# A two-layer attention block: the transfers of a unit's sums get a list of their own, and one load of layer 1's cross attention stands two rounds later

## The chip, the cores and the metric

The kernel runs on one core of a Trainium2 chip. The metric is the device time of one execution in microseconds; shown are the median and the spread of three runs. TensorE is called PE below, VectorE DVE, ScalarE ACT, GpSimd POOL and SyncE SP, as in the profile. SP computes nothing here: it issues the DMA transfers, one after the other, and a transfer whose data or buffer isn't ready holds up all that stand behind it.

## The reference

Input are x (4 batches of 512 tokens of 320 values) and a context (4 batches of 1601 tokens of 192 values), all in fp32. Two layers of the same form, with their own weights, follow each other. Of a layer, cut to what matters (20 heads of 16 values):

```
h1 = ln(x);  x = attn(h1, h1)      + x      # self attention, 512 keys
h2 = ln(x);  x = attn(h2, context) + x      # cross attention, 1601 keys
h3 = ln(x);  a, g = split(h3 @ ff_w1 + ff_b1)
x  = (a * gelu(g)) @ ff_w2 + ff_b2 + x

attn: q, k, v from wq, wk, wv;  softmax(q k^T / 4) v;  then @ wo + bo
```

## The kernel before, in words

**Units.** The work is cut into units. One unit of attention is a layer, a kind (self or cross), a batch b (0 to 3) and a group g of four heads (0 to 4, the 20 heads in fives of four). So each layer has 20 self units, then 20 cross units, then four feed-forward units, one for each batch. A unit takes its keys in chunks of 128: 4 chunks for self attention, 13 for cross attention (the last with 65 keys). For each chunk PE makes the scores of the four heads transposed (`st`, L1324), ACT takes the exponential into `pr` (L1334), and PE multiplies it with the values (`av`, L1350). The sums of the first chunk are copied to `o` by ACT (L1364); those of each later one are copied to `vo` (L1369) and added to `o` by POOL (L1370). The values have a column of ones, so `o` holds the softmax's denominators too. There are two `o` buffers, used in turn.

**Maxima one unit ahead.** While one unit is computed, PE also makes the scores of the next unit untransposed (`sps`, L1076 and L1101), and DVE takes their maxima (L1087, L1111). Two chunks before the unit ends the maxima are put together and transposed (`turned`, L1163), and four small transfers take them to `nrows` (L1171). The third `st` product of the next unit subtracts them, so its first chunk can't be finished before `nrows` has landed.

**The order of the work.** Nothing is scheduled by the chip: a planner in the kernel's Python code writes all instructions in one order, and each engine does its own in that order. It counts rounds: a chunk is two rounds. At each round it looks at the heads of several lists (`chains`), first in, first out, each entry with a due round and with conditions on rounds. `pick` takes, among the heads that may go, the one with the smallest due round, and the list's name decides between equal ones. The lists are for dividing, projecting, normalising and so on. Entries that cost PE time are also held back by a credit that is filled at an even pace. Transfers of queries and keys (L876) and of normalised rows (L595) come from lists of another kind and follow the picked work of a round.

**What follows a unit.** When a unit's last chunk is done, `add_finish` puts `turn` (L1191) in a list. It writes `o` from the chip to a buffer in memory (`oway`), 256 KB. After the fifth group of a batch, `sums` reads the denominators back (L1199), DVE inverts them, they are written out (L1208), and `read` loads numerators `aT` and inverse denominators `rT` (L1224, L1225) in three parts of 112, 112 and 96 rows; POOL multiplies them (`divide`, L1232). `rT` has two buffers: the third `rT` load waits until POOL has done the first division. Both of `turn` and of the divisions stand in the list "divide", so a `turn` waits in that list behind divisions and loads of the batch before. The third load may go when a number of rounds has passed since the second load: seven in layer 0, five in layer 1. Then comes the third division, and after it the projection with `wo` in eight pieces of 12 matmuls (`ops`, L1250), which DVE adds to x (L1257).

**Feed-forward.** The last batch of a layer's cross attention is divided and projected during the first feed-forward units. A feed-forward unit makes two matrix products into `fps` (L1435 for 256 of the 320 rows, L1495 for the rest), ACT and DVE make `hid` from them (L1506, L1507), and four products `yps` of 128 tokens (L1542) are added to x by DVE (L1549) and, in layer 1, written out by SP (L1553). Its input is normalised by DVE, transposed in blocks, moved by SP to `hT` in 16 transfers (L595) and scaled by POOL (L612).

Of the kernel before, what the change touches and what calls it, by code (L numbers as in the profile page):

```python
# [78 lines left out]
def kernel(ctx: ExitStack, tc: tile.TileContext, x, context, ws, out):  # L79
# [313 lines left out]

    chains = {n: deque() for n in ("divide", "project", "norm", "scale", "context", "early", "proj", "values")}
    clock = {"round": 0, "credit": 0.0, "lights": 0, "tiles": None, "ff": False}
    ALIKE = ("project", "early", "proj", "values")
    LIGHT = 0.01
# [13 lines left out]
    def bank(name):  # L413
        i = min(range(NB), key=lambda i: bank_free[i])
        assert bank_free[i] < HELD, name
        t = psum.tile([P, 512], F32, tag=f"bank{i}", name=name)
        bank_of[id(t)] = [i, t, bank_free[i], 0.0]
        bank_free[i] = HELD
        return t

    def written(us, *tiles):
        expect["pe"] = max([expect["pe"]] + [bank_of[id(t)][2] + 0.05 for t in tiles]) + us
        for t in tiles:
            bank_of[id(t)][3] = expect["pe"] + 0.17

    def busy(engine, us, *tiles):
        expect[engine] = max([expect[engine]] + [bank_of[id(t)][3] + 0.05 for t in tiles]) + us
        for t in tiles:
            bank_free[bank_of[id(t)][0]] = expect[engine] + 0.09
# [12 lines left out]
    def add(chain, cost, f, due, ready=yes, soon=yes):  # L442
        chains[chain].append((cost if isinstance(cost, tuple) else (cost,), due, ready, soon, f))
# [356 lines left out]
    def tiles_of(n):  # L800
        return [(f, min(SLOT, n - f)) for f in range(0, n, SLOT)]

    held = {"open": 0, "written": 0, "read": 0}
# [375 lines left out]
    def add_finish(u):  # L1179

        when = [clock["round"]]

        def since(i, n):
            return lambda: len(when) > i and clock["round"] >= when[i] + n

        def turn():

            way = o_way[u.b % 2]  # L1190
            dma(out=way[:, u.g * HG : (u.g + 1) * HG].rearrange("s j n -> j s n"), in_=u.o)  # L1191
            if u.g == G - 1:
                held["written"] += 1
                errands.append((clock["round"] + 3, yes, sums))

        def sums():

            den = two.tile([P, N], F32, tag="rT", name="den")[:, : H * N // P]
            dma(out=den, in_=o_way[u.b % 2][DH].rearrange("h n -> (h n)").rearrange("(p c) -> p c", p=P))  # L1199
            when.append(clock["round"])  # L1200

            def invert():
                nc.vector.reciprocal(den, den)
                busy("dve", 0.75)
                when.append(clock["round"])

            def save():
                dma(out=r_way[u.b % 2].rearrange("h n -> (h n)").rearrange("(p c) -> p c", p=P), in_=den)  # L1208
                errands.append((clock["round"] + 3, lambda: held["open"] < 1, read))

            add("divide", LIGHT, invert, r - 20, yes, since(1, 3))
            add("divide", 0.0, save, r - 20, yes, since(2, 1))

        def read():

            held["read"] += 1
            held["open"] += 1
            aT = one.tile([P, 3, N], F32, tag="aT", name="aT")
            way, part = o_way[u.b % 2], {}

            def load(k, at, n):
                heads = slice(at // DH, (at + n) // DH)
                part[k] = two.tile([P, N], F32, tag="rT", name="rT")
                dma(out=aT[:n, k, :], in_=way[:DH, heads])  # L1224
                dma(  # L1225
                    out=part[k][:n],
                    in_=r_way[u.b % 2][heads].rearrange("(o j) n -> o j n", o=1).to_broadcast([DH, n // DH, N]),
                )
                when.append(clock["round"])

            def divide(k, n):
                nc.gpsimd.tensor_tensor(aT[:n, k, :], aT[:n, k, :], part[k][:n], ALU.mult)  # L1232

            for k, at, n in DK[:2]:
                load(k, at, n)
            first, second, third = DK
            add("divide", 0.0, lambda: divide(0, first[2]), r - 20, yes, since(4, 3))
            add("divide", 0.0, lambda: divide(1, second[2]), r - 20)
            add("divide", 0.0, lambda: load(*third), r - 20, yes, since(4, 5 if u.l else 7))
            add("divide", 0.0, lambda: divide(2, third[2]), r - 20, yes, since(5, 3))  # L1240
            add("divide", 0.0, lambda: end(aT), r - 20)

        def project(aT, t, part):
            cols = slice(part * D // 2, (part + 1) * D // 2)
            ps = bank("ops")
            written(0.93, ps)
            busy("dve", 0.3, ps)
            for k, at, n in DK:
                for f, m in tiles_of(P):
                    nc.tensor.matmul(  # L1250
                        ps[f : f + m, : D // 2],
                        lhsT=aT[:n, k, f * NQ + t * SLOT : f * NQ + t * SLOT + m],
                        rhs=wo[:n, k, cols],
                        start=(k == 0),
                        stop=(k == 2),
                    )
            nc.vector.tensor_tensor(xs[u.b][:, t, cols], ps[:, : D // 2], xs[u.b][:, t, cols], ALU.add)  # L1257

        def end(aT):
            now = clock["round"]  # L1260
            for t in range(NQ):
                for part in range(2):
                    add(
                        "project", (0.317,) * 3, lambda t=t, part=part: project(aT, t, part),
                        now + 2 + u.nch * t + u.nch // 2 * part, yes, lambda: clock["round"] >= now + 1,
                    )
            add("project", 0.0, done, now + 2 + u.nch * NQ)

        def done():
            held["open"] -= 1  # L1270
            after(u)

        r = when[0]
        add("divide", 0.0, turn, r - 20, lambda: u.g or held["written"] < held["read"] + 2, since(0, 2))


    late = []
# [33 lines left out]
    def main(u, give, nxt):  # L1311
# [31 lines left out]
        def values(c):  # L1343
            r = min(P, u.nkeys - c * P)
            if u.g in (0, 2):
                until(lambda: units[u.i - u.g].vmade[u.g // 2] > c, "values")
            ps = bank("av")
            for j in range(HG):
                head = (c * H + u.g * HG + j) * VW
                nc.tensor.matmul(  # L1350
                    ps[j * SLOT : (j + 1) * SLOT, :],
                    lhsT=columns_of[:r, head : head + SLOT],
                    rhs=pr.pop((c, j))[:r, :],
                    start=True,
                    stop=True,
                )
            u.valued = c + 1
            expect["pe"] = max(expect["pe"], raised[c] + 0.1)
            written(1.0, ps)
            busy("dve" if last else "act", 0.52, ps)  # L1360

            if c == 0:
                u.o = two.tile([P, N], F32, tag="o", name="o")
                (nc.vector.tensor_copy if last else nc.scalar.copy)(u.o, ps)  # L1364
            elif last:
                nc.vector.tensor_tensor(u.o, ps, u.o, ALU.add)
            else:
                vo = prs.tile([P, N], F32, tag="pr", name="vo")
                nc.scalar.copy(vo, ps)  # L1369
                nc.gpsimd.tensor_tensor(u.o, u.o, vo, ALU.add)  # L1370
            if c == u.nch - 1:
                add_finish(u)
# [214 lines left out]
    def after(u):  # L1587

        stage[u.b] += 1
        if u.b == B - 1:  # L1590
            load_bias(u.l, ("self", "cross", "ff").index(u.kind) + 2)
            if u.kind == "self":
                loads.extend(load_out(u.l, "o2_w"))
            if u.kind == "cross" and u.l + 1 < L:
                loads.extend(load_out(u.l + 1, "o1_w"))
            if u.l + 1 < L:
                if u.kind == "ff":
                    loads.extend(load_cross(u.l + 1))
                elif u.kind == "self":
                    loads.extend(load_self(u.l + 1))  # L1600
# [172 lines left out]
```

## Time and profile before

| | |
|---|---|
| median of 3 runs | 2929.41 us (2924.77 to 2933.03) |
| the profiled execution, its own time | 2929.68 us |
| its span, first to last instruction | 2927.9 us |
| PE busy, share of the span | 2863.1 us (98%) |
| DVE, ACT, POOL busy | 1980.7, 1950.1, 1299.5 us |
| DMA, mean over the span | 64 GB/s |
| cross attention, layer 0 and layer 1 | about 424 to 1206 us and 1871 to 2650 us |

The page of the profile gives busy time by engine, and the chain of work that ended last. The waits tell for each engine which instruction sat idle and which event ended it: "PE st L1324 <- DMA nrows<-turned: 7.0, 8, 1.6" reads 7.0 us in all, 8 times, the longest 1.6 us. The waits of SPq are those of the DMA issuing queue. A row of the timeline is a start, a length, the engine and line, and what is written from what; "x4" means that four instructions were merged in the row, and brackets at its end give idle time before it and what ended it. A row of SPq shows the issue of a transfer, not its landing.

### The profile page before, as it was taken

The numbers are of one execution on the slowest core, as the hardware profiler recorded it, in microseconds if no ns is written. First come the engines' busy times: TensorE is split into PE (matmuls) and PEld (weight loads), VectorE is DVE, ScalarE is ACT, GpSimd is POOL, SyncE is SP. The second block draws the span as 40 slices with busy tenths as digits, with TensorE's granted clock in tenths as the row PEclk, the third lists the DMA queues.
The fourth block names the chain that finished last, engine by engine and source line by source line (L and its number), as shares of the span: only waits on it lengthen the run. The fifth ranks groups of instructions, "written<-read, shape, count | busy, mean of one in ns | idle before, by whom it ended". The sixth has DMA issues, their size and how long they took to land.

```text
span 2927.9 us, 83288 instructions
## 1 busy us (share of the span) xinstructions
PE 2863.1 (98%) x35018; PEld 1545.3 (53%) x35018; DVE 1980.7 (68%) x3752; ACT 1950.1 (67%) x4033; POOL 1299.5 (44%) x1409
## 2 busy tenths in 40 slices
PE   8999999999999999999999999999999999999999
PEld 4445555555555555355554555555555555544554
DVE  7776878788788878323257678788778888762221
ACT  3777678887888888500138776788888888893000
POOL 3556345555555645211125653455455564451110
PEclk8999999999999999999999999999999999999999
DMA  3443224232232222200113432221122122122000
GB/s 106 111 123 98 67 71 105 59 82 63 51 92 62 54 54 62 84 18 11 36 44 88 109 98 66 68 65 49 54 65 50 47 72 63 42 59 72 20 23 14
DMA packets 163494, 188.59 MB, mean 64 GB/s; under 512 B 61988, under 2 KB 109104, under 8 KB 163120
## 3 DMA queue, kind: packets, MB, share of 16 engines
q1 hardware_dynamic: 162616, 181.69, 24.3%
q8 instruction: 275, 4.51, 0.6%
q10 hardware_dynamic: 472, 1.58, 0.2%
q14 instruction: 99, 0.81, 0.1%
q0 software_dynamic: 32, 0.00, 0.0%
HBM read 55.76 MB, written 29.36 MB: 29 GB/s over the span
## 4 chain that ended last, share of the span: by engine, by line
PE 85%; DVE 6%; POOL 4%; issue 2%; DMA 2%; ACT 1%; SPq 1%; POOLq 0%; ACTq 0%; DVEq 0%
PE av L1350 21%; PE st L1324 19%; PE fps L1435 10%; PE sps L1076 8%; PE yps L1542 6%; PE vps L1035 5%; PE ops L1250 3%; PE kps L972 3%; PE qkps L908 3%; PE fps L1495 3%; DVE nmax L1087 2%; DVE pm L1087 2%; PE qps L947 2%; POOL o L1370 1%; PE sps L1101 1%
## 5 line engine op out<-in xcount | busy, mean ns | idle before, releaser
L1334 ACT ACTIVATE pr<-st 128x512 f32<-128x512 f32 (+1 forms) x2720 | 1404.5, 604 | 327.1 <-PE st L1324 297.0
L1087 DVE TENSOR_REDUCE pm<-sps 128x1 f32<-128x512 f32 (+1 forms) x1920 | 1149.0, 660 | 251.0 <-PE sps L1076 243.8
L1370 POOL TENSOR_TENSOR o<-o,vo 128x512 f32<-128x512 f32 x576 | 739.8, 1284 | 936.9 <-ACT vo L1369 922.1
L1076 PE MATMUL sps<-kT,q 32*128 32x450 f32 (+1 forms) x4800 | 870.7, 422 | 10.7 <-DMA q<-halves 4.3
L1324 PE MATMUL st<-q,kT 32*128 32x512 f32 (+1 forms) x5120 | 791.1, 420 | 2.0 <-ACT o L1364 1.6
L1350 PE MATMUL av<-pr,vals 128*32 128x512 f32 (+1 forms) x5440 | 734.8, 606 | 30.7 <-DVE pm L1087 7.2
L1324 PEld LDWEIGHTS st<-q,kT 32*128 32x128 f32 (+1 forms) x5120 | 448.6, 180 | 293.9 <-ACT pr L1334 115.4
L1324 PE MATMUL st<-nrows,ones 32*128 32x512 f32 (+1 forms) x2720 | 560.8, 398 | 7.1 <-DMA nrows<-turned 7.0
L1087 DVE TENSOR_REDUCE nmax<-sps 128x1 f32<-128x512 f32 x640 | 397.2, 682 | 120.6 <-PE sps L1076 115.2
L1076 PEld LDWEIGHTS sps<-kT,q 32*128 32x128 f32 x4800 | 434.6, 184 | 69.5 <-ACT pr L1334 12.8
L1369 ACT COPY vo<-av 128x512 f32<-128x512 f32 x576 | 352.9, 613 | 15.2 <-PE av L1350 8.5
L1506 ACT ACTIVATE gl<-fps,b 128x512 f32<-128x512 f32 x80 | 54.7, 687 | 409.0 <-PE fps L1495 301.1
L1435 PE MATMUL fps<-hT,w 128*128 128x512 f32 x640 | 283.5, 597 | 0.0
L1324 PEld LDWEIGHTS st<-nrows,ones 32*128 32x128 f32 (+1 forms) x2720 | 263.3, 180 | 18.7 <-issue 6.2
L1350 PEld LDWEIGHTS av<-pr,vals 128*32 128x32 f32 (+1 forms) x5440 | 110.9, 108 | 304.3 <-DVE pm L1087 186.7
L1507 DVE SCALAR_TENSOR_TENSOR hid<-fps,b,gl 128x512 f32<-128x512 f32 x80 | 59.7, 748 | 247.5 <-ACT gl L1506 245.4
L1435 PEld LDWEIGHTS fps<-hT,w 128*128 128x128 f32 x640 | 119.1, 190 | 155.0 <-issue 152.3
L1542 PE MATMUL yps<-w,hid 128*128 128x320 f32 x640 | 175.7, 434 | 0.0
L1542 PEld LDWEIGHTS yps<-w,hid 128*128 128x128 f32 x640 | 120.5, 190 | 56.3 <-ACT gl L1506 5.3
L1250 PEld LDWEIGHTS ops<-wo,aT 112*32 112x32 f32 (+1 forms) x3072 | 97.9, 110 | 61.9 <-issue 30.0
L1250 PE MATMUL ops<-wo,aT 112*32 112x160 f32 (+1 forms) x3072 | 124.9, 300 | 4.1 <-POOL aT L1232 3.8
L1111 DVE TENSOR_REDUCE pm<-sps 128x4 f32<-128x508 f32 x160 | 98.9, 681 | 36.1 <-PE sps L1101 33.0
(89 smaller groups left out, 2459.5 us busy)
## 6 DMA issues: line engine op xcount, KB each, us to landing
kT<-stages SPq DMA_DIRECT2D x80, 400.5 KB
oway<-o SPq DMA_DIRECT2D x80, 256.0 KB
q<-halves SPq DMA_DIRECT2D x80, 256.0 KB
q<-halves SPq DMA_DIRECT2D x27, 512.0 KB
kT<-halves SPq DMA_DIRECT2D x40, 256.0 KB
aT<-oway SPq DMA_DIRECT2D x32, 224.0 KB
rT<-rway SPq DMA_DIRECT2D x32, 224.0 KB
hT<-hturned SPq DMA_DIRECT2D x96, 64.0 KB
```

The costliest lines, as they stand in the source:

```text
L1035: nc.tensor.matmul(ps[f : f + m, :w], lhsT=u.kvT[:n, k, at + f : at + f + m], rhs=wv[:n, k, h0 * DH : h1 * DH], start=(k == 0), stop=(k == ...
L1076: nc.tensor.matmul(own[0][:, :w], lhsT=u.queries(slice(j * SLOT, (j + 1) * SLOT), e, t), rhs=u.kT[j * SLOT : (j + 1) * SLOT, u.k0 + at : u ...
L1087: nc.vector.tensor_reduce(to, own[0][:, :w], AX.X, ALU.max)
L1111: nc.vector.tensor_reduce(u.pm[:, :, j, ns - 1], ps[:, : NQ * w].rearrange("p (t w) -> p t w", w=w)[:, :, :n], AX.X, ALU.max,)
L1250: nc.tensor.matmul(ps[f : f + m, : D // 2], lhsT=aT[:n, k, f * NQ + t * SLOT : f * NQ + t * SLOT + m], rhs=wo[:n, k, cols], start=(k == 0) ...
L1324: nc.tensor.matmul(own[0][:r, :], lhsT=ones[rows, :r] if e == 2 else u.keys(rows, c), rhs=u.rows[rows, :] if e == 2 else u.queries(rows, e ...
L1334: nc.scalar.activation(p[:r], own[0][:r], AF.Exp)
L1350: nc.tensor.matmul(ps[j * SLOT : (j + 1) * SLOT, :], lhsT=columns_of[:r, head : head + SLOT], rhs=pr.pop((c, j))[:r, :], start=True, stop= ...
L1369: nc.scalar.copy(vo, ps)
L1370: nc.gpsimd.tensor_tensor(u.o, u.o, vo, ALU.add)
L1435: nc.tensor.matmul(ps, lhsT=w1[:, k, i * FF + c * P : i * FF + (c + 1) * P], rhs=natural(u.hT[:, k]), start=start, stop=stop,)
L1542: nc.tensor.matmul(ps[:, :D], lhsT=hid[c][:, t * P : (t + 1) * P], rhs=w2[:, c, :], start=(c == 0), stop=(c == NHC - 1),)
```

## The change

Two edits.

First, `turn` gets a list of its own, "turn", in place of the list "divide". Its due round and its conditions are the same. The new list is named first in the table of lists; `pick` goes by due round and then by name, so the place in the table doesn't decide.

Second, the third load of `aT` and `rT` waits seven rounds instead of five after the second load in the cross units of layer 1. Layer 1's self units keep five, layer 0 keeps seven.

```
-    chains = {n: deque() for n in ("divide", "project", "norm", "scale", "context", "early", "proj", "values")}
+    chains = {n: deque() for n in ("turn", "divide", "project", "norm", "scale", "context", "early", "proj", "values")}
...
-            add("divide", 0.0, lambda: load(*third), r - 20, yes, since(4, 5 if u.l else 7))
+            add("divide", 0.0, lambda: load(*third), r - 20, yes, since(4, 5 if u.l and not u.cross else 7))
...
-        add("divide", 0.0, turn, r - 20, lambda: u.g or held["written"] < held["read"] + 2, since(0, 2))
+        add("turn", 0.0, turn, r - 20, lambda: u.g or held["written"] < held["read"] + 2, since(0, 2))
```

What the two edits do to the order of the instructions can be told apart. The first moves instructions on SP alone, at six places: three in layer 0's self attention and three in layer 1's, each time one `turn` that now stands in front of transfers it stood behind. The second moves the third load on SP, and from there on, in layer 1's cross attention and in its feed-forward units, the rounds in which projections, key and value products and norms are placed. The number of instructions of each kind stays the same.

The first of the six places, on SP, in layer 0's self attention (some 177 us into the span): `aT`, `rT` are batch 0's third load, `oway_131` is written by the `turn` of a unit of batch 1. L765 saves the transposed context to memory, L779 loads it from there; the lines between the two pieces are the same in both kernels, and the four `nrows` of the next unit are among them, behind four L779 loads.

```order
 L1225 DMA rT<-rway_132 96x1x512
+L1191 DMA oway_131<-o 4x32x512
 L765 DMA ctxT_126<-stages 768x1x32
 L779 DMA w_116<-ctxT_126 96x1x416 x2
...
 L779 DMA w_116<-ctxT_126 96x1x385 x2
-L1191 DMA oway_131<-o 4x32x512
 L876 DMA kT_101<-halves 128x1x512
```

The `turn` now stands in front of the last context save, the context loads and the `nrows` of the next unit.

The second place, on SP, in the same stage (some 265 to 275 us): the third load of batch 1, and the `turn` of a unit of batch 2.

```order
 L876 DMA q_102<-halves 128x1x1024
-L1171 DMA nrows_97<-turned 8x4x32 x4
-L1224 DMA aT<-oway_131 96x1x512
-L1225 DMA rT<-rway_133 96x1x512
-L876 DMA kT_101<-halves 128x1x512
-L876 DMA q_103<-halves 128x1x1024
-L1191 DMA oway_130<-o 4x32x512
+L1191 DMA oway_130<-o 4x32x512
+L1171 DMA nrows_97<-turned 8x4x32 x4
...
 L1191 DMA oway_130<-o 4x32x512
```

The `turn` now stands in front of eight transfers that it stood behind. At the other four places (some 344, 1631, 1719 and 1794 us) it changes places with the four `nrows` that stood in front of it.

The third load in layer 1's cross attention, on SP, batch 0 (some 2064 to 2080 us); batch 1 and batch 2 show the same exchange.

```order
 L1225 DMA rT<-rway_132 112x1x512
-L1224 DMA aT<-oway_130 96x1x512
-L1225 DMA rT<-rway_132 96x1x512
-L1171 DMA nrows_97<-turned 8x4x32 x4
+L1171 DMA nrows_97<-turned 8x4x32 x4
+L1224 DMA aT<-oway_130 96x1x512
+L1225 DMA rT<-rway_132 96x1x512
 L1191 DMA oway_131<-o 4x32x512
```

The four `nrows` of the next unit now stand in front of the third load.

Behind that, each piece of the projection comes one chunk later on PE, or two come together, and key and value products move by a chunk to make room. In the feed-forward units of layer 1 the eight projection pieces of batch 3 also come later: the last two stood in batch 2's unit between the two halves of 16 L1435 products, and now stand behind these and the 8 L1495 products that follow. On SP, the 16 `hT` transfers of batch 3 were all in front of batch 2's four output transfers; now six stand in front of the first output, six between the first and the second, and four between the second and the third.

## The prediction

> **What bounds the kernel now.** I read the page first (busy shares and the chain of work that ended last), then PE's waits over the whole span, then PE's waits in each layer's cross attention, then the timeline at every place where the order of the instructions changes.
>
> ```profile
> span 2927.9 us, 83288 instructions
> PE 2863.1 (98%) x35018; PEld 1545.3 (53%) x35018; DVE 1980.7 (68%) x3752; ACT 1950.1 (67%) x4033; POOL 1299.5 (44%) x1409
> PE 85%; DVE 6%; POOL 4%; issue 2%; DMA 2%; ACT 1%; SPq 1%; POOLq 0%; ACTq 0%; DVEq 0%
> PE st L1324 <- DMA nrows<-turned: 7.0, 8, 1.6
> ```
>
> PE is busy for 2863.1 of 2927.9 us, so all that a new order can win at most, with the same PE work, is 64.8 us of idle time, and most of that lies in places that the change doesn't touch. A change in the order pays by the PE waits it ends or makes, and by nothing else. One kind of wait fits the change: PE waits eight times for `nrows`, 7.0 us in all. Next come the waits of PE in layer 1's cross attention (first four rows, 1870 to 2655 us) and in layer 0's (last five rows, 424 to 1206 us).
>
> ```profile
> PE av L1350 <- DVE pm L1087: 3.9, 6, 1.2
> PE st L1324 <- DMA nrows<-turned: 2.8, 3, 1.1
> PE av L1350 <- ACT pr L1334: 0.8, 4, 0.2
> PE sps L1076 <- ACT pr L1334: 0.5, 1, 0.5
> PE av L1350 <- DVE pm L1087: 3.3, 2, 2.0
> PE av L1350 <- ACT pr L1334: 2.3, 10, 0.3
> PE sps L1076 <- DVE x L1257: 0.7, 1, 0.7
> PE av L1350 <- ACT vo L1369: 0.3, 1, 0.3
> PE st L1324 <- DMA nrows<-turned: 0.3, 1, 0.3
> ```
>
> The same attention is run twice, with five rounds behind the second load in layer 1 and seven in layer 0. With five, `nrows` is late three times, once each for batches 0, 1 and 2, for 2.8 us; with seven, once for 0.3 us. The waits sum to 8.0 us in layer 1 and 6.9 us in layer 0.
>
> **The third load, two rounds later.** Its place in batch 0, from SP, DVE, POOL and PE:
>
> ```profile
> 2064.63 0.60 SPq L1224 DMA_DIRECT2D aT<-oway  x1
> 2078.99 0.54 SPq L1225 DMA_DIRECT2D rT<-rway  x1
> 2079.64 2.65 SPq L1171 DMA_DIRECT2D nrows<-turned  x4
> 2076.60 0.21 DVE L1163 STREAM_TRANSPOSE turned<-nmax 128x32 f32<-128x32 f32 x1
> 2077.66 2.56 POOL L1232 TENSOR_TENSOR aT<-aT,rT 112x512 f32<-112x512 f32 x2
> 2083.49 0.49 PE L1324 MATMUL st<-nrows,ones 32*128 32x512 f32 x2 [0.86 <-DMA nrows<-turned]
> ```
>
> SP issues the third `aT` load and then stands for 13.8 us, from 2065.23 to 2078.99, until POOL's first division (2077.66 plus half of 2.56, so 2078.94) has freed an `rT` buffer. The maxima are ready at 2076.81, but their four transfers are behind that load: issued from 2079.64 to 2082.29, and PE goes on 1.2 us later, at 2083.49, after 0.86 us idle. With the change the four stand in front: issued from 2076.85 to 2079.5, usable 1.2 us later, at 2080.7. PE wants them at 2082.63, so they have 1.9 us to spare, and the wait ends. The third load then finds its buffer free since 2078.94, so SP doesn't stand there at all. The three batches give the row's 2.8 us.
>
> What the later load delays is the third division on POOL and the projection behind it: each piece comes a chunk later. Nothing waits for these soon; batches 0 to 2 are next read in the feed-forward. PE has the same products to do and fills the chunk with key and value products that were to come later. This costs nothing as long as DVE keeps pace with the new mix, and layer 0 with its seven rounds is the nearest row for it: its DVE waits are 3.3 us against 3.9. So I take -2.8 us. The bounds: -1.1 us, if layer 1 ends with layer 0's sum of waits (8.0 - 6.9), and -8.0 us, if the new mix ended every wait of that stage.
>
> **The `turn` at the second place (some 265 us): a gain.**
>
> ```profile
> 264.68 1.28 POOL L1370 TENSOR_TENSOR o<-o,vo 128x512 f32<-128x512 f32 x1 [0.70 <-ACT vo L1369]
> 268.94 2.64 SPq L1171 DMA_DIRECT2D nrows<-turned  x4
> 274.63 0.78 SPq L1191 DMA_DIRECT2D oway<-o  x1
> 284.51 0.59 ACT L1364 COPY o<-av 128x512 f32<-128x512 f32 x1 [4.22 <-DMA oway<-o]
> 285.14 0.73 PE L1324 MATMUL st<-q,kT 32*128 32x512 f32 x3 [1.64 <-ACT o L1364]
> SPq L1199 <- DMA oway<-o: 48.3, 10, 5.2
> ```
>
> ACT's copy into `o` waits 4.22 us until the transfer out of the same buffer, issued at 274.63, has landed; PE loses 1.64 us by it. The sums were ready at 264.68 + 1.28 = 265.96, but the `turn` stood behind eight transfers. With the change it stands in front of `nrows`, which weren't ready before 268.94; it goes at about 266, 8.6 us earlier, and ACT's 4.22 us are gone. It holds up nothing: 0.78 us of issue end before 268.94. So -1.6 us. The other bound is 0, because the releaser of ACT's wait is inferred: a transfer of 9.9 us from issue to release is long beside the 5.2 us at most that the denominators' load waits for such a write.
>
> The Trainium skill, "DMA: Bandwidth & Descriptors", section "Anatomy of one DMA", has a fit for transfers that GpSimd issues, about 2.0 us plus the bytes at 436 GB/s; as an estimate from that page, 256 KB would land 2.6 us after the issue, at 277.2 us, before ACT began to wait at 280.29. By that rule the wait isn't this transfer's, this term is 0, and the whole sum below would be -0.4 us instead of -2.0. The trace speaks against it with its 4.22 us and 5.2 us, and I go by the trace.
>
> **The `turn` at the first place (some 177 us): a loss.**
>
> ```profile
> 177.05 0.57 SPq L1225 DMA_DIRECT2D rT<-rway  x1
> 177.72 0.56 SPq L765 DMA_DIRECT2D ctxT<-stages  x1
> 181.11 3.48 SPq L779 DMA_DIRECT2D w<-ctxT  x4
> 184.69 2.66 SPq L1171 DMA_DIRECT2D nrows<-turned  x4
> 179.66 1.28 POOL L1370 TENSOR_TENSOR o<-o,vo 128x512 f32<-128x512 f32 x1
> 191.75 1.27 POOL L1232 TENSOR_TENSOR aT<-aT,rT 96x512 f32<-96x512 f32 x1
> 188.45 0.50 PE L1324 MATMUL st<-nrows,ones 32*128 32x512 f32 x2 [1.12 <-DMA nrows<-turned]
> 193.08 0.62 PE L1250 MATMUL ops<-wo,aT 96*32 96x160 f32 x12 [2.11 <-POOL aT L1232]
> ```
>
> Here the `turn` moves to 177.7 us, but POOL adds to its sums until 180.94. SP stands there, issues it (0.78) and goes on with L765 at 181.7 instead of 177.72: 4.0 us later. L779 reads back what L765 wrote, 3.4 us after its issue, and the four `nrows` are behind L779; PE already waits 1.12 us for them. All this comes 4.0 us later, or 5.9 us, if the 256 KB in front make L765's data land as late as a `turn` does (5.2 us after the end of its issue, at 182.3, makes L779 start near 187.0-187.5, against 181.11). But PE's next wait takes in part of it: at 193.08 PE has lost 2.11 us to a division that ends at 193.02 and isn't behind the delayed work. That wait goes. Net: 4.0 - 2.1 = 1.9 us to 5.9 - 2.1 = 3.8 us. I take 2.4 us, near the low end, since the 3.4 us are this very transfer's. Without that cover it would be the full 4.0 to 5.9 us. The context loads, key and query transfers behind `nrows` shift too, but are for units a batch or several chunks away.
>
> **The other four places.** There `turn` only changes places with `nrows`. At three of them the sums are ready before the maxima, so nothing changes. At the fourth they aren't:
>
> ```profile
> 1633.27 2.67 SPq L1171 DMA_DIRECT2D nrows<-turned  x4
> 1633.44 1.29 POOL L1370 TENSOR_TENSOR o<-o,vo 128x512 f32<-128x512 f32 x1
> 1642.53 0.39 PE L1324 MATMUL st<-nrows,ones 32*128 32x512 f32 x1
> ```
>
> SP waits until 1634.73, issues 0.78, and starts `nrows` at 1635.5, 2.2 us later; they end at 1638.2 and are usable at 1639.4, 3.1 us before PE wants them. Cost 0, with that cover; 2.2 us at most if it weren't there.
>
> **The feed-forward.** Batch 3's last projection pieces come later, and its `hT` transfers are split by batch 2's outputs, each of which waits for DVE's addition:
>
> ```profile
> 2848.17 0.49 DVE L1549 TENSOR_TENSOR x<-yps,x 128x320 f32<-128x320 f32 x1 [4.89 <-PE yps L1542]
> 2858.74 1.45 PE L1435 MATMUL fps<-hT,w 128*128 128x512 f32 x3
> 2865.70 3.70 PE L1495 MATMUL fps<-hT,w1r 64*128 64x512 f32 x16
> ```
>
> The last four stand behind the second output, so they go after 2848.66, at some 2.7 us of issue by the pace of `nrows`, so end near 2852; with 5.2 us to land that is 2857, and PE wants that part of `hT` at 2865.70, the others at 2858.74. Cost 0, with some 8 us of cover.
>
> **The sum.** -2.8 - 1.6 + 2.4 = -2.0 us against the profiled execution's 2929.68 us: 2927.7 us. The median of the runs, 2929.41, is 0.27 us lower, so I predict **2927.4 us**. The runs lie between 2924.77 and 2933.03; less than 0.3% (8.8 us) can hardly be told from no change.
>
> **The rivals.**
>
> *Faster still.* The new mix in layer 1 also ends the DVE waits: -8.0 - 1.6 + 2.4 = -7.2 us, 2922.2 us. For it: six short waits of DVE there, all tied to where small DVE work falls between maxima. Against it: layer 0, with nearly this mix, has 3.3 us of them.
>
> *Slower: the first place isn't covered.* SP's stand for POOL at 177.7 us delays `nrows` by 5.9 us, and PE's later wait doesn't shrink, because POOL's division slips with PE. With the gains at their lower bounds (-1.1 and 0) that is +4.8 us, 2934.2 us. It decides from the point where the net loss there exceeds the 4.4 us gained elsewhere. For it: SP is in order, and a 256 KB write goes ahead. Against it: the division at 191.75 stands on POOL behind work that comes from products before the wait.
>
> *Slower: the feed-forward.* If batch 3's `hT` landed some 8 us later than worked out, PE would stand at 2858.74 or 2865.70; each product group there lasts 5.4 us (from one addition's 4.89 us wait and its 0.49), and one such step makes -2.0 + 5.4 = +3.4 us, 2932.8 us. Against it: the 8 us of cover.
>
> *The change does less than it says.* The list's place in the table decides nothing, and only six of 80 `turn`s move. If both moves of `turn` come to nothing and another wait takes the place of `nrows` (DVE's, in the same chunk), the time stays at 2929.4 us.
>
> **How the numbers follow.** I give the forecast 0.60, the faster rival 0.10, the uncovered first place 0.12, the feed-forward 0.05, no effect 0.13. Nearly all of these lie within 0.3% (2920.6 to 2938.2). Faster by over 0.3% needs the faster rival and more, or a lucky set of runs: 0.07. Slower by over 0.3% needs one slow rival dearer than its price: 0.05. Same: 0.88. The range reaches from the faster rival less 2 us of the runs' spread, 2920, to the slower one, 2934.5.
>
> **What would show it.** Right: among the waits, PE's `nrows` waits near 2083, 2293 and 2503 us are gone, and SP's waits for `aT` behind the third `rT` load in that stage nearly so; ACT's 4.22 us and PE's 1.64 us near 284 us are gone; near 188 us PE's `nrows` wait is 5 to 7 us and its 2.11 us wait for the division gone. Wrong: new PE waits for DVE in layer 1's cross attention, PE idle at the start of the last feed-forward unit, or an `nrows` wait near 188 us that stays at 1.1 us.

## The result, and the profile after

| | before | changed |
|---|---|---|
| median of 21 runs | 2929.41 us (2921.93 to 2933.03) | 2922.3 us (2917.78 to 2925.17) |
| ratio, 95% interval | | 0.9975 (0.9969 to 0.9981) |
| the profiled execution | 2929.68 us | 2922.84 us |
| its span | 2927.9 us | 2921.1 us |

The change makes the kernel 7.1 us faster, by the interval of the ratio 5.6 to 9.1 us. That is under 0.3% and inside the forecast range, but it is 5 us more than the forecast of 2.0 us, and it is the time of the rival called "faster still" (2922.2 us); how much of that is luck is told further down.

First the page of the changed kernel (span, busy times, shares of the chain that ended last) and from PE's waits over the whole span the row of `nrows`.

```profile
span 2921.1 us, 83291 instructions
PE 2859.9 (98%) x35018; PEld 1545.5 (53%) x35018; DVE 1975.7 (68%) x3752; ACT 1950.2 (67%) x4033; POOL 1299.7 (44%) x1409
PE 87%; DVE 4%; POOL 3%; DMA 2%; issue 2%; ACT 1%; SPq 1%; POOLq 0%; ACTq 0%; DVEq 0%
PE st L1324 <- DMA nrows<-turned: 9.6, 5, 5.8
```

The row of `nrows` has grown from 7.0 to 9.6 us, but it now stands in one large wait of 5.8 us. In the chain, DVE's share has fallen from 6% to 4%: here is a first sign that the gain isn't where the forecast put it. PE's waits in layer 1's cross attention (1870 to 2655 us), after the change:

```profile
PE av L1350 <- DVE pm L1087: 1.0, 3, 0.6
PE av L1350 <- ACT pr L1334: 0.9, 4, 0.2
PE st L1324 <- DMA nrows<-turned: 0.4, 1, 0.4
```

Their sum is 2.3 us, where it was 8.0. `nrows` lost 2.4 of its 2.8 us, as forecast. But DVE's row lost 2.9 of its 3.9 us, and ACT's 0.5 us is gone. How much of the stage that is, the windows show. Each is cut at the first product of the 65-key chunk at the end of a batch; the sum row gives the length of the four stretches and PE's busy time in them, of before and then of after. The row above the second sum is one of its four stretches; behind the counts it has the granted clock of TensorE (1.00 is full speed).

```profile
sum 779.59, PE 767.29 PEld 419.01 DVE 609.56 ACT 664.83 POOL 413.71; mean PE 191.82 PEld 104.75 DVE 152.39 ACT 166.21 POOL 103.43
```

```profile
2078.70:2287.36 208.66, 207.12 (x3000) 115.40 (x2997) 167.01 (x306) 178.62 (x379) 114.13 (x109) 1.00 0.22 57
sum 772.63, PE 766.47 PEld 419.34 DVE 605.37 ACT 664.26 POOL 413.63; mean PE 191.62 PEld 104.84 DVE 151.34 ACT 166.07 POOL 103.41
```

The stage is 6.96 us shorter: 6.1 us less of PE idle (779.59 - 767.29 = 12.3 against 772.63 - 766.47 = 6.2) and 0.8 us less of busy time. The granted clock is 1.00 in the row shown and in all eight stretches, so it isn't the clock. This one stage gains as much as the whole difference of the medians. The two places in layer 0's self attention come on top, one dearer than forecast and one cheaper.

**What DVE had waited for.** The rows of a batch are normalised while the batch ahead of it is in cross attention. For that DVE takes three tiny steps of an inverse root on 128x4 numbers (L521, L522, L525), and POOL does the rest of it. Near 2131 us, for batch 2's norm, the kernel before shows, from POOL, DVE and PE:

```profile
2129.76 1.89 POOL L828 TENSOR_TENSOR stages<-stages 128x801 f32<-128x801 f32 x1
2131.66 1.29 POOL L1370 TENSOR_TENSOR o<-o,vo 128x512 f32<-128x512 f32 x1
2131.16 0.52 DVE L521 TENSOR_SCALAR root<-mv 128x4 f32<-128x4 f32 x1
2131.72 1.26 DVE L522 TENSOR_SCALAR root<-root 128x4 int32<-128x4 int32 x1
2133.01 0.17 DVE L525 TENSOR_SCALAR root<-root 128x4 int32<-128x4 int32 x1
2133.76 1.07 PE L1350 MATMUL av<-pr,vals 128*32 128x512 f32 x8 [1.17 <-DVE pm L1087]
```

Three instructions of the same size take 0.52, 1.26 and 0.17 us. The first ends at 2131.68, where POOL's L828 ends (2131.65); the second ends at 2132.98, where POOL's L1370 ends (2132.95). DVE's maxima behind them are late, and PE stands for 1.17 us. The same happens at 2341 us (1.17 us of PE) and once more at 2557 us, where L525 takes 1.27 us under a single L1370 (0.60 us of PE): 2.94 us in all, just what DVE's row lost. The same place in the changed kernel:

```profile
2126.89 1.28 POOL L1370 TENSOR_TENSOR o<-o,vo 128x512 f32<-128x512 f32 x1 [2.10 <-ACT vo L1369]
2130.02 1.28 POOL L1370 TENSOR_TENSOR o<-o,vo 128x512 f32<-128x512 f32 x1 [1.84 <-ACT vo L1369]
2132.18 1.90 POOL L828 TENSOR_TENSOR stages<-stages 128x801 f32<-128x801 f32 x1
2129.51 0.16 DVE L521 TENSOR_SCALAR root<-mv 128x4 f32<-128x4 f32 x1
2129.71 0.17 DVE L522 TENSOR_SCALAR root<-root 128x4 int32<-128x4 int32 x1
```

Now the root falls between two of POOL's additions, its steps take 0.16 and 0.17 us, and PE's wait is gone. At this norm and at the one near 2341 us nothing has been moved past the root on DVE. It is POOL's two steps on a key product (L827, L828) that stand one chunk later, since the key products moved to make room for the later projection: in POOL's order, ten entries of L1370 now stand between them and the key product ahead, where nine did. At the third place one addition of DVE (L1257), which stood ahead of the root, now stands behind it, and the root is done before POOL's L1370 starts.

The Trainium skill states a lock of this kind: by "SBUF — State Buffer", section "Who interferes with whom", VectorE and GpSimd share a port pair, a scalar operation of VectorE on SBUF can take it, and whoever comes second is fully blocked until the other's instruction ends. The ends 2131.68 against 2131.65 and 2132.98 against 2132.95 agree with that. By the same section a reduction never asks for the pair; DVE's L1087 goes on at 2.42 us for four while POOL runs in both kernels, so here too the traces agree.

**The first place in layer 0's self attention.** From SP and PE of the changed kernel, and from SP's waits between 172 and 194 us:

```profile
177.74 0.60 SPq L1191 DMA_DIRECT2D oway<-o  x1
178.43 0.54 SPq L765 DMA_DIRECT2D ctxT<-stages  x1
184.32 2.50 SPq L779 DMA_DIRECT2D w<-ctxT  x4
190.74 0.79 PE L1324 MATMUL st<-nrows,ones 32*128 32x512 f32 x2 [5.78 <-DMA nrows<-turned]
SPq L779 <- DMA ctxT<-stages: 5.3, 1, 5.3
```

This profiled execution reaches the place 3.2 us earlier than the one of before: an `av` product ahead of it, which no edit has touched, starts at 168.69 and not at 171.87. With that taken off, the `turn` goes at 180.9 and L765 at 181.6, just as worked out. But L779 goes 5.9 us after L765's issue, not 3.4: behind the 256 KB the small write lands late. That is what the prediction took as its upper bound.

PE's wait is not all that this place costs. While PE stands, the granted clock falls: it is 0.50 from 189.09 to 195.92 us, and 1.00 throughout in the kernel before. So the products behind the wait take longer. The windows reach from the product that waited to the start of the next chunk's `st`, in the changed kernel and then in the kernel before; the `av` rows, in the same order, are the next ones behind them.

```profile
190.74:197.52 6.78, 6.78 (x93) 3.87 (x94) 1.94 (x4) 2.65 (x5) 2.50 (x3) 0.62 0.75 207
188.45:195.12 6.67, 4.56 (x92) 2.89 (x92) 2.00 (x5) 2.65 (x5) 6.58 (x8) 1.00 0.64 160
199.04 1.06 PE L1350 MATMUL av<-pr,vals 128*32 128x512 f32 x8
196.66 1.07 PE L1350 MATMUL av<-pr,vals 128*32 128x512 f32 x8
```

The same products keep PE busy for 6.78 us in place of 4.56. From the `av` at 168.69 to the one at 199.04 it is 30.35 us, where the kernel before needs 24.79 (171.87 to 196.66): the place costs 5.56 us. Of these the waits are 5.78 - 1.12 - 2.11 = 2.55 us and the slower products 2.2 us; most of the rest is a wait of 0.66 us for `nrows` at 171.09, which this execution has ahead of the moved `turn`. PE's waits alone thus show less than half of the loss. In all four traces with this order (here, and in three experiments below) the clock falls at this place; in the kernel before, and in the three others that leave this `turn` in its place and the root on DVE, it doesn't.

**The second place.** ACT's copy near 284 us, and the `turn` in front of it, in the changed kernel:

```profile
268.38 0.60 SPq L1191 DMA_DIRECT2D oway<-o  x1
282.53 0.62 ACT L1364 COPY o<-av 128x512 f32<-128x512 f32 x1
```

The `turn` goes as soon as the sums are ready (here at 267.07 + 1.28 = 268.35). This execution is 2.4 us later at this place, so that is the 8.6 us earlier that the prediction worked out, and neither ACT's copy nor PE waits there any more. From one `av` to the next it is 5.12 us (281.33 to 286.45) where it was 7.60 (278.94 to 286.54): 2.5 us won, of which 1.64 us are the wait.

### The profile page after: what moved, and what is told of

It reads as the page before. It is cut to its first block, busy times and chain, and to the rows that moved or that the text cites. A ratio compares the mean times of both kernels' runs of the same rounds, so it can differ in the third digit from the quotient of the medians.

```text
span 2921.1 us, 83291 instructions
## 1 busy us (share of the span) xinstructions
PE 2859.9 (98%) x35018; PEld 1545.5 (53%) x35018; DVE 1975.7 (68%) x3752; ACT 1950.2 (67%) x4033; POOL 1299.7 (44%) x1409
## 4 chain that ended last, share of the span: by engine, by line
PE 87%; DVE 4%; POOL 3%; DMA 2%; issue 2%; ACT 1%; SPq 1%; POOLq 0%; ACTq 0%; DVEq 0%
PE av L1350 22%; PE st L1324 20%; PE fps L1435 10%; PE sps L1076 9%; PE yps L1542 6%; PE vps L1035 5%; PE kps L972 4%; PE ops L1250 3%; PE qkps L908 3%; PE fps L1495 3%; DVE nmax L1087 2%; PE qps L947 2%; PE sps L1101 1%; POOL o L1370 1%; DVE pm L1087 1%
## 5 line engine op out<-in xcount | busy, mean ns | idle before, releaser
L1087 DVE TENSOR_REDUCE pm<-sps 128x1 f32<-128x512 f32 (+1 forms) x1920 | 1148.5, 660 | 248.3 <-PE sps L1076 242.6
L1370 POOL TENSOR_TENSOR o<-o,vo 128x512 f32<-128x512 f32 x576 | 739.9, 1285 | 935.4 <-ACT vo L1369 918.8
L1087 DVE TENSOR_REDUCE nmax<-sps 128x1 f32<-128x512 f32 x640 | 397.0, 682 | 121.5 <-PE sps L1076 112.1
L1435 PE MATMUL fps<-hT,w 128*128 128x512 f32 x640 | 283.1, 597 | 0.0
L1435 PEld LDWEIGHTS fps<-hT,w 128*128 128x128 f32 x640 | 119.2, 190 | 155.1 <-issue 152.2
```

The lines of the kernel that those rows point to most:

```text
L1087: nc.vector.tensor_reduce(to, own[0][:, :w], AX.X, ALU.max)
L1435: nc.tensor.matmul(ps, lhsT=w1[:, k, i * FF + c * P : i * FF + (c + 1) * P], rhs=natural(u.hT[:, k]), start=start, stop=stop,)
```

## The experiments

Two theories stood against each other. **A:** most of what the forecast lacked is DVE's root being held by POOL's running instruction; moving the key products took it out of POOL's way. **B:** the gain comes from the place of the projection's pieces and products alone, or from the `turn`s, and DVE's waits went for other reasons. For each kernel the ratio is to the kernel before on the same chip, whose median there was 2928.61 us for the first four, 2928.54 us for the next three and 2931.63 us for the last. The ratio isn't the quotient of these medians and can differ from it by some 0.001; an interval in us is worked out from that of the ratio.

### Each edit alone

The first edit alone:

```
-    chains = {n: deque() for n in ("divide", "project", ...
+    chains = {n: deque() for n in ("turn", "divide", "project", ...
...
-        add("divide", 0.0, turn, ...
+        add("turn", 0.0, turn, ...
```

> The first edit alone (turn in a list of its own; the third load as before). Theory A (gain and loss of the turns are those traced in the changed kernel): at the first place PE waits 5.8 us for nrows in place of 1.1 and 2.1, so 2.5 us lost; at the second 1.6 us won; nothing elsewhere: 0.9 us slower than before, ratio 1.0003, and layer 1's cross attention keeps its three nrows waits (2.8 us) and its DVE waits (3.9 us). Theory B (the turns carry the unforeseen part of the gain, by freeing SP earlier in layer 1): 3 us or more faster than before, and fewer waits in layer 1.

Measured: 2932.49 us, ratio 1.0011 (1.0002 to 1.002), so 3.9 us more than before, with an interval of 0.6 to 5.9 us. PE's waits from 150 to 424 us (first row), its wait at the first place, and the window behind it:

```profile
PE st L1324 <- DMA nrows<-turned: 8.4, 2, 6.6
192.30 0.79 PE L1324 MATMUL st<-nrows,ones 32*128 32x512 f32 x2 [6.64 <-DMA nrows<-turned]
192.30:199.12 6.82, 6.82 (x93) 3.90 (x93) 1.94 (x4) 2.65 (x5) 2.59 (x4) 0.61 0.74 208
```

At the first place PE's wait grows from 1.12 to 6.64 us, the wait of 2.11 us ends, and the products behind it take 6.82 us again, at a granted clock of 0.61. From the `av` ahead of the place (170.30) to the one behind it (200.65) it is 30.35 us, to the hundredth as in the changed kernel: 5.56 us lost. The second place gains its 2.5 us. That makes 3.1 us of loss, inside the interval. Theory A had the sign right but expected 0.9 us, since it took the loss at the first place by the waits alone; theory B's gain is excluded. The rest, 0.8 us, is less than what single executions differ by where nothing was moved: near 659 us DVE waits 2.82 us for a context transfer to leave its buffer and PE 1.8 us behind it, and that wait of DVE is 1.00 us in the kernel before, 1.83 us in the changed kernel and 1.00 us in a kernel below with the same two edits. The first edit as a whole is a loss, and layer 1's cross attention is untouched by it (3.9 us of waits for DVE, 2.9 for `nrows`).

The second edit alone:

```
-            add("divide", 0.0, lambda: load(*third), r - 20, yes, since(4, 5 if u.l else 7))
+            add("divide", 0.0, lambda: load(*third), r - 20, yes, since(4, 5 if u.l and not u.cross else 7))
```

> The second edit alone (third load seven rounds behind in layer 1's cross attention; turn in its old list). Theory A: the whole of the 7 us comes from layer 1's cross attention, which is 7.0 us shorter; so 7 to 8 us faster than before, ratio 0.9974, with PE's waits there 2.3 us in place of 8.0, and the first and second place as before (1.1 and 2.1 us, 1.6 us). Theory B: half of the gain needs the first edit, 3 to 4 us faster.

Measured: 2920.84 us, ratio 0.9976 (0.9965 to 0.9986), so 7.8 us less. Its waits in layer 1's cross attention:

```profile
PE av L1350 <- DVE pm L1087: 1.0, 3, 0.5
PE av L1350 <- ACT pr L1334: 0.9, 4, 0.2
```

1.9 us in place of 8.0: the whole gain of the change, in one edit, and the stage is 7.25 us shorter than before (772.34 us between the first and the last of the cuts used above). This is what A expected; B's 3 to 4 us lie just outside the interval (4.1 to 10.3 us). The first place has its old wait. At the second place PE waits 2.26 us for ACT's copy, 1.64 in the trace of before, and here the granted clock falls behind it:

```profile
286.41:289.82 3.41, 3.41 (x44) 2.13 (x40) 0.83 (x2) 1.10 (x3) 1.87 (x2) 0.50 0.14 44
```

So the same order can cost more at this place in one execution than in another.

### Both edits, the new list at the second place alone

```
-        add("divide", 0.0, turn, ...
+        add("turn" if u.l == 0 and not u.cross and u.b == 2 else "divide", 0.0, turn, ...
```

> The changed kernel, but with the list of its own for layer 0's self units of batch 2 alone: the second place keeps its gain, at the first place the turn is behind the context loads again. Theory A: 2.5 us faster than the changed kernel, 9.7 us faster than before, ratio 0.9967; nrows wait near 188 us 1.1 us again. Theory B (the loss near 188 us is made good elsewhere): as the changed kernel, 7.1 us faster than before.

Measured: 2918.61 us (2917.26 to 2925.64), ratio 0.9968 (0.9956 to 0.9981): some 10 us less than before, with an interval of 5.6 to 12.9 us from five runs. That doesn't tell A's 9.7 us from B's 7.1, nor this kernel from the changed one; the trace does the former. Its waits from 150 to 424 us show the first place as it was, with the division's wait in place, and no wait for ACT's copy into `o`:

```profile
PE st L1324 <- DMA nrows<-turned: 3.1, 3, 1.7
PE ops L1250 <- POOL aT L1232: 1.6, 1, 1.6
```

So, by the trace, the second place's gain can be had without the first place's loss.

### The root's steps on POOL, with the order of before

```
-        nc.vector.tensor_scalar(a, var, EPS, None, ALU.add)
-        nc.vector.tensor_scalar(z.bitcast(I32), a.bitcast(I32), 1, None, ALU.logical_shift_right)
-        nc.vector.tensor_scalar(y.bitcast(I32), z.bitcast(I32), -1, 0x5F3759DF, ALU.mult, ALU.add)
+        eng.tensor_scalar(a, var, EPS, None, ALU.add)
+        eng.tensor_scalar(y.bitcast(I32), a.bitcast(I32), -0.5, float(0x5F3759DF), ALU.mult, ALU.add)
```

> The kernel before, with the order of both edits as before, but the three small DVE instructions at the start of a norm's inverse root (L521, L522, L525) done by GpSimd in two: the shift of the integer is a product with -0.5 of the integer read as a number, so the first guess is rounded otherwise. Theory A (PE's waits for DVE come from these small instructions, which DVE holds until a GpSimd instruction under way has ended): the DVE waits of PE go from 3.9 to about 1 us in layer 1's cross attention and from 3.3 to about 0 us in layer 0's, with the 2.8 us of nrows kept: 6 us faster than before, ratio 0.9980. Theory B (they come from the mix of projection and key and value pieces in a chunk): 3.9 and 3.3 us stay, same time as before.

Measured: 2924.46 us, ratio 0.9982 (0.9973 to 0.9992), 4.1 us less than before. Its waits in layer 1's cross attention (first two rows) and in layer 0's (last):

```profile
PE st L1324 <- DMA nrows<-turned: 2.8, 3, 1.1
PE av L1350 <- DVE pm L1087: 1.4, 3, 0.9
PE av L1350 <- DVE pm L1087: 1.5, 2, 1.2
```

The third load stays five rounds behind, and `nrows` and ACT (1.3 us) keep their waits. DVE's go from 3.9 to 1.4 us in layer 1 and from 3.3 to 1.5 us in layer 0, where A had expected about 1 and about 0 us; the interval of the time is 2.3 to 7.9 us, which takes in A's 6 us and leaves out B's none. So the waits hang on the root, in both layers, without any product being moved. This is what speaks most clearly for A and against B.

In layer 0 a hold costs more than the row of waits says. Near 688 us in the kernel before two steps in a row are held (1.44 and 1.19 us), PE waits 2.01 us, and the granted clock is 0.50 behind that:

```profile
690.70:694.10 3.40, 3.40 (x36) 1.84 (x32) 1.32 (x3) 0.90 (x2) 1.80 (x9) 0.50 0.47 91
```

With the root on POOL there is neither the wait nor the lower clock.

### The same with the other orders

The changed kernel with the root on POOL (the edit just shown):

> The changed kernel with the inverse root on GpSimd (first guess as in root_on_pool). If the changed kernel has already won what the root cost in layer 1: against the changed kernel only layer 0's collisions are left to win, DVE waits there 3.3 + 0.7 us to about 1.5, so 2.5 us less: 2919.8 us (2918.5 to 2921). If the root's place had nothing to do with the change's gain, the full 4.1 us of root_on_pool come on top: 2918.2 us. Layer 1's DVE waits stay at 1.0 us by the first theory.

Measured: 2920.57 us, ratio 0.9971 (0.9961 to 0.9981). And the kernel of the second place alone, with the root on POOL:

> The kernel before with the third load seven rounds behind in layer 1's cross attention, with the turn list only for layer 0's self units of batch 2, and with the inverse root on GpSimd (as in root_on_pool: the first guess of the root is a product with -0.5 in place of a shift, so it rounds differently). If DVE's waits come from its root being held by a running POOL instruction: layer 1's cross attention keeps its 1.0 us of DVE waits (the roots were already out of POOL's way there), layer 0's go from 3.3 + 0.7 us to about 1.5 us, so some 2.5 us less than place2_only's 2918.6 us: 2916 us (2914.5 to 2917.5). If root_on_pool's gain came from something else that layer 1's new order already has: no gain, 2918.6 us. If the gains simply add (8 of the seven rounds, 2 of the second place, 4 of the root): 2914.5 us.

Measured: 2917.92 us, ratio 0.9956 (0.9942 to 0.997), the fastest here, though it can't be told from 2918.61. The first of the two times lies within what A gives; the second, from five runs, lies 0.4 us above A's range and nearer to "no gain", so the times alone decide nothing. And one part of A's expectation failed: DVE's waits in layer 1 were to stay at 1.0 us and are 2.8 us in both kernels. The place, in the changed kernel with the root on POOL:

```profile
2137.36 1.44 POOL L577 TENSOR_SCALAR hn<-x,mv,root 128x320 f32<-128x320 f32 x1
2138.84 0.51 DVE L585 STREAM_TRANSPOSE hturned<-hn 128x320 f32<-128x320 f32 x1 [1.28 <-POOL hn L577]
2139.91 1.06 PE L1350 MATMUL av<-pr,vals 128*32 128x512 f32 x8 [0.93 <-DVE pm L1087]
```

and in the changed kernel:

```profile
2140.33 0.51 DVE L585 STREAM_TRANSPOSE hturned<-hn 128x320 f32<-128x320 f32 x1 [0.54 <-POOL hn L577]
2141.40 1.06 PE L1350 MATMUL av<-pr,vals 128*32 128x512 f32 x8 [0.20 <-DVE pm L1087]
```

POOL's chain for the root has two more steps, the normalised rows (`hn`) come 0.7 us later, and DVE, which does its work in order, stands 1.28 instead of 0.54 us for them with maxima behind. So the root on POOL wins layer 0's collisions and gives part of it back in layer 1, where the new order had left none that PE waited for. Between the first products of the same 65-key chunks, layer 0's cross attention takes 777.39 us in place of the changed kernel's 781.61, and layer 1's 774.56 us in place of 772.63: 4.2 us won, 1.9 us given back.

### The root moved in time, everything still on DVE

The gate on the root, set here in the changed kernel and then in the kernel before:

```
-            busy("dve", 0.65)
+            busy("dve", 0.65); s["stats"] = clock["round"]
...
-                (lambda: clock["round"] > s["round"]) if step else yes,
+                (lambda: clock["round"] > s["round"]) if step else (lambda: not (l == 1 and i == 1 and b > 1) or clock["round"] >= s["stats"] + 3),
```

> The changed kernel, with the inverse root in layer 1's cross attention held back three rounds behind the last statistics, for batches 2 and 3 alone (the two norms that fall at some 2337 and 2552 us); nothing is left out. If DVE's waits come from a root that falls under POOL's long addition of the transposed rows or the sums: the roots fall next to POOL's work of the next chunk again, single instructions of 0.5 to 1.3 us in place of 0.16 to 0.17, and PE's wait for DVE's maxima in that stage goes from 1.0 us to 2 to 3.3 us; the time 1 to 2.5 us over the changed kernel's. If the waits came from the order of the projection pieces and not from the root's place: the wait stays near 1.0 us and the time within 0.5 us.

Measured: 2922.7 us, ratio 0.9977 (0.9968 to 0.9986), the same as the changed kernel. The two norms that the gate holds back are those of batches 2 and 3, near 2130 and 2337 us in the changed kernel; the expectation named the wrong pair. Their roots did go under POOL's L828 again, but only under its end:

```profile
2134.89 1.91 POOL L828 TENSOR_TENSOR stages<-stages 128x801 f32<-128x801 f32 x1
2136.03 0.79 DVE L521 TENSOR_SCALAR root<-mv 128x4 f32<-128x4 f32 x1
2136.86 0.17 DVE L522 TENSOR_SCALAR root<-root 128x4 int32<-128x4 int32 x1
2137.82 1.07 PE L1350 MATMUL av<-pr,vals 128*32 128x512 f32 x8 [0.34 <-DVE pm L1087]
```

L521 is held for 0.6 us, until 2136.82 (POOL ends at 2136.80), and the next step is free, since no L1370 follows at once. PE loses 0.34 us in place of the 1.17 us that a hold by two instructions in a row costs. The expected 1 to 2.5 us didn't come: the hold is there, its price was set too high. PE's waits for DVE in this stage are 1.3 us, 1.0 in the changed kernel, and the stage is 0.7 us longer (773.33 us). By time and row this run came out as the other theory said, and only the single instructions speak for A.

In the kernel before:

> The kernel before, with the inverse root in layer 1's cross attention held back three rounds behind the last statistics of a batch's norm, from batch 2's norm on; nothing is left out, the third load stays five rounds behind. In the kernel before POOL has nothing to do at the new place (some 2133 to 2139 us but for the root's own chain). If DVE's waits come from the root under POOL's L828 and L1370: its instructions take 0.16 to 0.17 us each again near 2136 and 2344 us, PE's two waits of 1.17 us for DVE's maxima shrink to 0.3 us or less, the row goes from 3.9 to between 1.5 and 2.5 us, the row of nrows stays near 2.8 us, and the time is 1.5 to 2.5 us under the kernel before's. If the waits came from the place of the projection's pieces: two waits of about 1 us stay and the time is the kernel before's.

Measured: 2927.06 us, ratio 0.9988 (0.9978 to 0.9998). This trace shows both cases within one execution. Batch 2's norm, which came clear of POOL, and then batch 3's, which did not, from DVE, POOL and PE:

```profile
2136.93 0.16 DVE L521 TENSOR_SCALAR root<-mv 128x4 f32<-128x4 f32 x1
2137.12 0.17 DVE L522 TENSOR_SCALAR root<-root 128x4 int32<-128x4 int32 x1
2341.56 1.91 POOL L828 TENSOR_TENSOR stages<-stages 128x801 f32<-128x801 f32 x1
2343.43 1.26 POOL L1370 TENSOR_TENSOR o<-o,vo 128x512 f32<-128x512 f32 x1
2342.24 1.26 DVE L521 TENSOR_SCALAR root<-mv 128x4 f32<-128x4 f32 x1
2343.53 1.19 DVE L522 TENSOR_SCALAR root<-root 128x4 int32<-128x4 int32 x1
2345.50 1.07 PE L1350 MATMUL av<-pr,vals 128*32 128x512 f32 x8 [1.83 <-DVE pm L1087]
```

Near 2137 us POOL has nothing running, the steps take 0.16 and 0.17 us, and the old wait of 1.17 us is gone. Near 2342 us the root has come under L828 and L1370 once more; its two steps take 1.26 and 1.19 us, end with POOL's two instructions (2343.50 against 2343.47, 2344.72 against 2344.69), and PE waits 1.83 us. DVE's row is 2.8 us, not the 1.5 to 2.5 us expected, because the delay cleared the one collision and made the other worse. The stage is 1.7 us shorter (777.87 us); the medians differ by 4.6 us, with an interval of 0.6 to 6.4 us, so the time tells little. The pair of places shows what the wait depends on: where the root falls in POOL's work, and by how much of it.

## Why the prediction was right, and where it was wrong

The direction held and the time lies in the range, but the sum was 5 us short: all three of its terms were too small, two gains and one loss. That the measured time is the rival's 2922.2 us to 0.1 us is luck: the rival adds -8.0, -1.6 and +2.4, where the two traces give -7.0, -2.5 and +5.6.

- **The third load (-2.8 us): right in mechanism, too small.** `nrows` went in front as worked out (issued from 2077.16, with the division off SP's way), and its waits fell by 2.4 us. The sentence that failed is "This costs nothing as long as DVE keeps pace with the new mix, and layer 0 with its seven rounds is the nearest row for it". It put the change in DVE's waits at nothing. DVE didn't keep the pace of layer 0: its waits fell from 3.9 to 1.0 us, because three of them, 2.94 us in sum, came from collisions between root and POOL and not from the mix. The stage gained 6.96 us by the windows: 2.4 for `nrows`, 2.9 for DVE, 0.5 for ACT, 0.8 of PE's busy time, and the rest in small gaps. The bound of -8.0 us held.
- **"Faster still".** Its words were right ("The new mix in layer 1 also ends the DVE waits"), and so was what was said for it (waits "tied to where small DVE work falls between maxima"). What spoke against it, layer 0's 3.3 us, did not count: layer 0 has its own collisions, which go with the root (3.3 to 1.5 us). The trace of before had the row that would have told: three DVE steps of one size with 0.52, 1.26 and 0.17 us.
- **The first place (+2.4 us): right in mechanism, too small.** The wait of 5.78 us (6.64 us with the first edit alone) and the end of the 2.11 us wait were predicted. The step "I take 2.4 us, near the low end, since the 3.4 us are this very transfer's" failed: behind 256 KB that transfer took 5.9 us from issue to the load behind it. The upper bound, 5.9 - 2.1 = 3.8 us, failed too: the place costs 5.56 us in both traces, because the sum counted PE's waits alone and put the clock at nothing, and the products behind the wait took 2.2 us more at 0.50. This is more than the 4.4 us from which the rival "the first place isn't covered" was to decide. The cover that this rival doubted was there; the kernel didn't get slower because the third load gained 7.0 us and not 2.8.
- **The second place (-1.6 us): right in mechanism, too small by 0.9 us in these two traces.** ACT's and PE's waits are gone, and the stretch is 2.5 us shorter. Here the estimate from the Trainium skill, "DMA: Bandwidth & Descriptors", section "Anatomy of one DMA", a fit for transfers that GpSimd issues, by which the wait wasn't this transfer's, didn't hold for this one of SP's: the wait went when the transfer was issued 8.6 us earlier.
- **The other four places and the feed-forward (0): right** as far as the windows tell. From the last cut at the end of layer 1's cross attention to the end of the span it is 2921.1 - 2643.80 = 277.3 us, against 2927.9 - 2650.43 = 277.5.

By the two traces the terms give -7.0 + 5.6 - 2.5 = -3.9 us; the medians give -7.1, with an interval of 5.6 to 9.1 us. Some 3 us are thus not accounted for, and their cause stays open. Single executions differ by as much: the `av` ahead of any edit starts at 168.69, 170.30 and 171.87 us in three traces, over the first 168 us the granted clock is 0.96 in the changed kernel's trace and 0.93 in that of before, and the second place costs more in the trace of the second edit alone than in that of before. So a pair of profiles can't place them.

## What to carry to other kernels

When a term is held to be free "as long as an engine keeps pace", look first at what that engine waits for now: instructions of one size with different durations are a wait inside the instruction, and no list of waits names it. When products are moved, follow what other engines do for them too; here 2.3 us of the gain (two waits of 1.17 us) came from two POOL steps that stood a chunk later. A small transfer that something waits for should not be issued right behind a large one: at the first place the large write cost twice what the second place won. And when a wait is priced, the granted clock behind it belongs to the price: measure from a product ahead of the wait to one well behind it, not the wait alone.

## What the runs showed of the hardware

- A DVE step on 128x4 numbers, 0.16 to 0.17 us alone, takes up to 1.44 us (L521 near 687 us) while POOL runs an instruction of 1.3 to 1.9 us, and ends 0.02 to 0.03 us after it. Where POOL starts its next instruction at once, the next DVE step is held by that one too: two holds cost PE a wait of 1.17 to 2.01 us, one hold of 0.6 us cost it 0.34 us.
- Behind PE's wait of 5.78 us the granted clock was 0.50 until 195.92 us, and behind waits of 2.01 and 2.26 us it was 0.50 for 3.4 us; products then took longer (6.78 in place of 4.56 us). Behind the waits of 1.17, 1.64 and 1.83 us told of here it stayed at 1.00. Where the limit lies these runs don't show.
- One wait for a context transfer (DVE, near 658 us) took between 1.00 and 2.82 us in kernels that don't differ there.
- A context write that is followed by a load of the same memory lets that load go 3.4 us after the write's issue, and 5.8 to 5.9 us after it when 256 KB are written just in front of it (first edit alone, changed kernel).
